# The last tile's 20 nodes: four copies in row quarters of the array in the last attention, and high and low parts stacked in one product of the sums

## The chip, the cores and the metric

The kernel runs on one core of a Trainium2 chip. The metric is the device time of one execution in microseconds (us). Before the change the median of three runs is 2953.96 us (2953.91 to 2956.05).

A core has a matrix engine, TensorE (PE in the profile; PEld is its loading of the fixed operand), a vector engine, VectorE (DVE), a scalar engine, ScalarE (ACT), and a general one, GpSimd (POOL). SyncE (SP) issues DMAs, as ACT and POOL also do. Each engine works through its own queue in order. A product on PE contracts over up to 128 rows, and its result goes to one of the accumulator banks.

## The reference, cut to what matters

Four graph layers on 2708 nodes with 512 features, and one adjacency matrix. Each layer's result is added to its input and normalized.

```python
# layer 0: mean over the first 64 neighbours, two linear maps
keep = Ab & (jnp.cumsum(Ab.astype(jnp.int32), axis=1) <= neibor_num)
nb_sum = keep.astype(X.dtype) @ X
xj = leaky_relu(nb_mean @ W_nb.T + b_nb);  xi = leaky_relu(X @ W_line.T + b_line)
# layer 1: mean over all neighbours, then linear maps
agg = mask @ x / jnp.maximum(deg, 1.0)
# layers 2 and 3: attention with 8 heads; layer 3 has a second attention with one head and an MLP
e = jax.nn.leaky_relu(src[:, :, None] + dst[:, None, :], ALPHA)
e = jnp.where(adj_mask[None, :, :], e, NEG)
attn = jax.nn.softmax(e, axis=-1)
return jnp.einsum('hnm,hmo->hno', attn, Wh)
...
h2 = _gat_heads(x1, mask, Wo[None], ao[None])[0]
out = jax.nn.relu(jax.nn.elu(h2) @ lin1_w + lin1_b) @ lin2_w + lin2_b
```

## The kernel before, in words

The 2708 nodes are cut into 22 tiles: 21 of 128 and a last one of 20 (`few` in the code, `LAST` its number). The transposed mask `maskT` lies in memory as [128 rows, 22 tiles, 2816 columns] of one-byte numbers: row and tile say which neighbour, the column says which node. In the last tile only 20 of 128 rows hold neighbours; the rest are zero.

Stage 0a (0 to 208 us of the profiled span): for each tile t the rows of x are transposed and multiplied by two weights. The first product is what the sums will add up; `keep_y` (L226) splits it into a rounded high part `yH` (ACT, L229) and the remainder `yL` (DVE, L230), both in a reduced format that PE multiplies faster. The second product becomes `u`, stored by POOL (L336). Beside this, 14 mask tiles are loaded by POOL (L257, kept one or two ahead), counted on ACT (L262), cut to 64 neighbours by prefix sums on DVE (L268, L271), transposed on PE (L280) and written by ACT into `maskT` as signs (`turn`, L284). Helper `product` (L232) multiplies; `pe()` fixes the order of PE in this stage.

Stage 0b (208 to 484): the first sums over neighbours (L478). Output tiles go in blocks (tiles 20 and 21 first, then 0 to 3, 4 to 7 and so on). For each neighbour tile j ACT casts a block's mask (`kT`, L351, two buffers) and PE multiplies it by yH and by yL of tile j, for each of the block's tiles into its own bank; there are four such banks. At the block's end ACT copies the banks out (L491). The other 8 masks are prepared between these products.

Stage 1 (484 to 867): the same for layer 1. First the products for yH, yL (L244) with `keep_y`, then per output tile one bank and 22 x 2 products (L529), with masks cast by ACT in three groups (L526). In this stage the last tile's product takes a path of its own (L234 to L242): four products into four column quarters (L237), added up by `groups4`, a matrix that adds four groups of 32 rows (L241).

The attentions with heads follow (to about 2121). Then the projection of the last attention (`project`, L585, without heads): PE multiplies (L643), ACT forms the exponentials `ecol` and `ucol` (L664, L665) and scales the rows into `R2` (L676). POOL then loads the weights of the MLP (L1012, L1013).

The last attention (`last_attention`, L1083) goes over six quads of output tiles (five of 512 columns, one of 148). For each neighbour tile j DVE makes the weights `e` (L722, four buffers) and adds them, scaled, into `acc` (L1101, L1103), and PE multiplies them with the four 128-column parts of R2 into four banks `pn` (L1097). At a quad's end ACT and DVE copy two banks each (L1118, L1116), PE adds up acc over rows (`den`, L1120), DVE takes the reciprocal (L1022), normalizes and applies elu (L1024, L942 to L945), and PE computes the MLP of this quad (L1046, L1071) between the next quad's tiles.

In all these loops the last tile costs PE as much as a full one. Already before the change, the attentions with heads put a second copy of the last tile's 20 rows at rows 32 to 51 (`TWIN` = 32), for which one DMA copies the mask's rows (L567).

The instructions are put into each engine's queue by a scheduler; except where `pe()` or `issue_after` ties them, their order on an engine is not fixed by the text.

Of the kernel before, what the change touches and what calls it, by code (L numbers as in the profile page):

```python
# [9 lines left out]
F32 = mybir.dt.float32  # L10
# [3 lines left out]
AF = mybir.ActivationFunctionType  # L14
OP = mybir.AluOpType
AX = mybir.AxisListType
# [14 lines left out]
def kernel(  # L31
# [18 lines left out]
    def rows(t):  # L50
        return min(P, N - t * P)
# [41 lines left out]


    few = N - (NT - 1) * P
    groups4 = const.tile([P, 32], F32, name="groups4")
    nc.vector.tensor_reduce(groups4, ident.rearrange("p (g n) -> p n g", g=4), AX.X, OP.add)
    assert few <= 32

    behind = []  # L100
# [100 lines left out]
    with ExitStack() as phase:  # L201
# [25 lines left out]

        def keep_y(t, n, pm):
            highs[t] = nc.scalar.copy(yH[:n, t, :], pm[:n])  # L229
            return nc.vector.tensor_sub(yL[:n, t, :], pm[:n], yH[:n, t, :].bitcast(F32))  # L230

        def product(xT, n, w, which, order=as_it_comes, pm=None):  # L232
            pm = ps_mm.tile([P, D], F32, name=f"pm{which}") if pm is None else pm
            if n == few and order is as_it_comes:  # L234
                nc.gpsimd.memset(xT[:, :, n:32], 0.0)
                for k in range(KD):
                    nc.tensor.matmul(pm[32 * k:32 * k + 32], xT[:, k, :32], w[:, k, :], start=True, stop=True)  # L237
                u = sm.tile([P, D], F32, name="u")
                nc.scalar.copy(u, pm)
                pm = sums()  # L240
                nc.tensor.matmul(pm[:few], groups4[:, :few], u, start=True, stop=True)  # L241
                return pm  # L242
            for k in range(KD):
                order(nc.tensor.matmul(pm[:n], xT[:, k, :n], w[:, k, :], start=(k == 0), stop=(k == KD - 1)))  # L244
            return pm


# [25 lines left out]
        def turn(i, m, psum, order=as_it_comes):  # L273
            t, n = turns[i], rows(turns[i])
            for g0 in range(0, NT, G):
                g1 = min(g0 + G, NT)
                ps = psum()
                for j in range(g0, g1):
                    w = rows(j)
                    order(nc.tensor.transpose(ps[:w, j - g0, :n], m[:n, j * P:j * P + w], identb[:n, :n]))  # L280
                parts = [(P, g0, min(g1, FULL))] + ([(rows(FULL), FULL, NT)] if g1 > FULL else [])
                for w, a, b in parts:
                    if a < b:
                        nc.scalar.activation(maskT[:w, a:b, t * P:t * P + n], ps[:w, a - g0:b - g0, :n], AF.Sign,  # L284
                                             saturate=False)
                yield

        def rows_of(src):
# [55 lines left out]
        with ExitStack() as ph:  # L344
# [123 lines left out]
            for i, b in enumerate(cuts):  # L468
                ts_ = range(*b)
                pa = {t: sums() for t in ts_}  # L470
                for j in range(NT):
                    if j + 1 < NT:
                        nxt, nxt_made = kept(b, j + 1)
                    elif i + 1 < len(cuts):
                        nxt, nxt_made = kept(cuts[i + 1], 0)
                    for t in ts_:
                        for y in (yH, yL):
                            nc.tensor.matmul(pa[t], kT[:, (t - b[0]) * P:(t - b[0] + 1) * P], y[:, j, :],  # L478
                                             start=(j == 0 and y is yH), stop=(j == NT - 1 and y is yL))
                    kT = nxt  # L480
                    if j % 3:
                        next(todo, None)
                    with tc.issue_after(nxt_made.ins):
                        next(both, None)
                with tc.issue_after(nxt_made.ins):
                    reciprocals(slice(*b))
                us = {}
                for t in ts_:
                    n = rows(t)
                    us[t] = st.tile([P, D], F32, name=f"u{t - b[0]}")  # L490
                    nc.scalar.activation(us[t][:n], pa[t][:n], AF.Copy, scale=rkeep[:n, t:t + 1])  # L491
                todo = finish(ts_, us)
# [23 lines left out]
        with ExitStack() as ph:  # L516
            st = ph.enter_context(tc.tile_pool(name="l1b", bufs=2))
            for t in range(NT):
# [4 lines left out]
                for g0 in range(0, NT, G):  # L523
                    g1 = min(g0 + G, NT)
                    mf = st.tile([P, G, P], F32R, name="mf")
                    nc.scalar.copy(mf[:, :g1 - g0, :], maskT[:, g0:g1, t * P:(t + 1) * P])  # L526
                    for j in range(g0, g1):
                        for y in (yH, yL):
                            nc.tensor.matmul(pa, mf[:, j - g0, :], y[:, j, :],  # L529
                                             start=(j == 0 and y is yH), stop=(j == NT - 1 and y is yL))  # L530
                u = sm.tile([P, D], F32, name="u")
                nc.vector.scalar_tensor_tensor(u[:n], pa[:n], rdeg[:n, t:t + 1], z1, op0=OP.mult, op1=OP.add)
                nc.vector.scalar_tensor_tensor(u[:n], u[:n], 0.0, x1, op0=OP.max, op1=OP.add)
# [29 lines left out]
        nc.vector.tensor_reduce(pick_c[:, g], rows_c, AX.X, OP.add)  # L563


    LAST, TWIN = NT - 1, 32
    nc.sync.dma_start(maskT[TWIN:TWIN + few, LAST, :N], maskT[:few, LAST, :N])  # L567
    ucol = late.tile([P, NT, H], F32, name="ucol")
    ecol = late.tile([P, NT, H], F32, name="ecol")
    for c in (ucol, ecol, vcol, bcol):  # L570
# [17 lines left out]
    def project(name, source, layer, v_dram, cuts, turned=None, first=None):  # L588
# [12 lines left out]
        with ExitStack() as ph:  # L601
# [24 lines left out]
            for t in range(NT):  # L626
# [8 lines left out]
                if twice:  # L635
                    nc.gpsimd.memset(xT[:, :, n:TWIN], 0.0)
                    nc.gpsimd.tensor_copy(xT[:, :, TWIN:TWIN + n], xT[:, :, :n])
                elif t == LAST:
                    nc.gpsimd.memset(R2[TWIN:2 * TWIN, LAST, :], 0.0)
                m = TWIN + n if twice else n  # L640
                for k in range(KD):
                    for a in range(2):
                        nc.tensor.matmul(pm[a][:m, :D // 2 + heads], xT[:, k, :m], w[:, k, a, :D // 2 + heads],  # L643
# [17 lines left out]
                            nc.vector.tensor_mul(view(R2[at, t, a * D // 2:(a + 1) * D // 2]), view(pm[a][at, :D // 2]),  # L661
                                                 ecol[at, t, a * hh + k:(a + 1) * hh:2, None].to_broadcast([n, hh // 2, HO]))
                else:
                    nc.scalar.activation(ecol[:n, t, :heads], d, AF.Exp, scale=ALPHA)  # L664
                    nc.scalar.activation(ucol[:n, t, :heads], d, AF.Exp, scale=1.0 - ALPHA)  # L665
                with tc.issue_after(scaled[t - 1].ins) if first and t else nullcontext():
                    made = first(t) if first else None
                for a in range(0 if twice else 2):
                    to, src = R2[:n, t, a * D // 2:(a + 1) * D // 2], pm[a][:n, :D // 2]
                    if heads > 1:  # L670
                        with tc.issue_after(made.ins) if made else nullcontext():
                            scaled[t] = nc.vector.tensor_mul(to.rearrange("p (h o) -> p h o", h=hh),
                                                             src.rearrange("p (h o) -> p h o", h=hh),
                                                             ecol[:n, t, a * hh:(a + 1) * hh, None].to_broadcast([n, hh, HO]))
                    else:
                        scaled[t] = nc.scalar.activation(to, src, AF.Copy, scale=ecol[:n, t, 0:1])  # L676
                if heads > 1:
                    nc.scalar.activation(vcol[:n, t, :], b[:n, :], AF.Exp, scale=ALPHA - 1.0)
                    nc.gpsimd.tensor_scalar(bcol[:m, t, :], ucol[:m, t, :], -STEP * (1.0 + 2.0 ** -22), None,
# [404 lines left out]
    def last_attention(ph, att, last):  # L1084
# [4 lines left out]
        for b, (t0, t1) in enumerate(quads):  # L1089
# [4 lines left out]
            for j in range(NT):  # L1094
                e = att.weights(b, 0, j, v)
                for k in range(KD):
                    nc.tensor.matmul(pn[k][:, :w], R2[:, j, k * P:(k + 1) * P], e[:, :w],  # L1097
                                     start=(j == 0), stop=(j == NT - 1))

                if j == 0:  # L1100
                    nc.vector.tensor_scalar(acc[:, :w], e[:, :w], ecol[:, j, 0:1], None, op0=OP.mult)  # L1101
                else:
                    nc.vector.scalar_tensor_tensor(acc[:, :w], e[:, :w], ecol[:, j, 0:1], acc[:, :w],  # L1103
                                                   op0=OP.mult, op1=OP.add)

                if b == 1 and j == 4:
# [361 lines left out]
```

## Time and profile before

| what | us |
| --- | --- |
| median of three runs | 2953.96 |
| lowest and highest run | 2953.91, 2956.05 |
| span of the profiled execution, first to last instruction | 2955.5 |
| stage 0a, to 208.2: PE busy | 193.3 |
| 484.5 to 647.4 (products of layer 1): PE busy | 158.6 of 162.9 |
| 866.9 to 2121.0 (attentions with heads): PE busy | 1220.2 of 1254.1 |
| 2121.0 to 2238.7 (projection of the last attention): PE busy | 113.4 of 117.7 |
| 2910.0 to 2955.5 (the end): PE busy | 31.2 of 45.5 |

The profiled execution has no time of its own beside its span; it lies 1.5 us above the median of the runs. The mean granted clock of PE is 0.995 of full speed. In a row of the profile, the line number is that of the kernel, then come engine, operation, output and inputs by name, shapes and count; in brackets stands how long the engine was idle before and what ended that. Matmuls are pipelined, so the spacing of their starts is shorter than the duration of one.

### The profile page before, as it was taken

What the parts mean: (1) busy time and instruction counts of PE and PEld (TensorE: products, weight loads), DVE (VectorE), ACT (ScalarE), POOL (GpSimd) and SP (SyncE); (2) the same over time, 40 slices, a digit from 0 to 9 for tenths busy, and PEclk for the clock granted to TensorE, in tenths of its full rate; (3) what the DMA queues carried; (4) which work ended last, traced back from release to release, by engine and by line L of the source; (5) the groups of instructions that cost most, each with busy time, mean ns of one, the idle gap of its engine ahead of it and who ended that gap; (6) DMA issues with size and microseconds to landing.
All of it is one profiled execution on the core that took longest, in us unless ns stands there. A gap on an engine that the chain in (4) does not pass through costs nothing. (4 is left out here: it accounts for less than half of the span.)

```text
span 2955.5 us, 36461 instructions
## 1 busy us (share of the span) xinstructions
PE 2874.1 (97%) x14398; PEld 1606.6 (54%) x14398; DVE 1998.5 (68%) x2408; ACT 1515.0 (51%) x1759; POOL 207.4 (7%) x344
## 2 busy tenths in 40 slices
PE   8999999999999999999999999999999999999998
PEld 4557766458888343444466433444475555555555
DVE  5866637543334999999977999999953434444342
ACT  3646532113223999999965999999951000000001
POOL 1101101101110000000022000000000010000001
PEclk9999999999999999999999999999999999999999
DMA  4633426322222111111143111121161000000000
GB/s 128 130 87 72 107 79 185 118 65 86 83 72 82 35 40 39 38 45 44 35 138 134 40 40 39 41 65 37 33 157 61 4 25 15 25 15 16 15 20 22
DMA packets 121152, 185.59 MB, mean 63 GB/s; under 512 B 41741, under 2 KB 66562, under 8 KB 120972
## 3 DMA queue, kind: packets, MB, share of 16 engines
q1 hardware_dynamic: 91808, 121.57, 13.8%
q0 software_dynamic: 18160, 57.39, 6.8%
q10 hardware_dynamic: 11004, 4.22, 0.6%
q8 instruction: 115, 1.88, 0.3%
q14 instruction: 65, 0.53, 0.1%
HBM read 153.10 MB, written 44.65 MB: 67 GB/s over the span
## 5 line engine op out<-in xcount | busy, mean ns | idle before, releaser
L722 DVE SCALAR_TENSOR_TENSOR e<-v_bc,ucol,maskT 128x1408 f32<-128x1408 f32 (+3 forms) x804 | 1135.9, 1469 | 327.6 <-PE pn L1097 314.4
L749 ACT ACTIVATE c<-e,bcol 128x1300 fp8e4<-128x1300 f32 (+1 forms) x688 | 965.8, 1423 | 65.4 <-DVE e L722 21.8
L916 PE MATMUL po<-e,R 128*64 128x512 f32 (+2 forms) x4224 | 907.8, 549 | 30.2 <-DVE e L722 27.3
L916 PEld LDWEIGHTS po<-e,R 128*64 128x64 f32 x4224 | 343.0, 137 | 561.9 <-issue 387.2
L1097 PE MATMUL pn<-e,R 128*128 128x512 f32 (+1 forms) x1056 | 413.4, 542 | 0.0
L1097 PEld LDWEIGHTS pn<-e,R 128*128 128x128 f32 x1056 | 191.0, 190 | 199.3 <-issue 196.1
L1048 ACT ACTIVATE w<-pl,b 128x256 f32<-128x256 f32 (+1 forms) x88 | 41.0, 466 | 372.8 <-PE pl L1046 364.7
L478 PE MATMUL acc<-yH,kT 128*128 128x512 f32 x484 | 197.4, 408 | 4.6 <-ACT kT L351 4.6
L478 PE MATMUL acc<-yL,kT 128*128 128x512 f32 x484 | 189.2, 391 | 0.0
L529 PE MATMUL acc<-yH,mf 128*128 128x512 f32 x484 | 188.4, 389 | 0.0
L529 PE MATMUL acc<-yL,mf 128*128 128x512 f32 x484 | 188.3, 389 | 0.0
L643 PE MATMUL pm<-w,xT 128*128 128x264 f32 (+1 forms) x704 | 167.5, 391 | 2.4 <-POOL ln_rs L120 0.8
L244 PE MATMUL pm<-weight,xT 128*128 128x512 f32 (+1 forms) x344 | 158.3, 603 | 7.6 <-DVE u L334 6.8
L1046 PE MATMUL pl<-lin 128*128 128x256 f32 (+1 forms) x704 | 153.4, 371 | 3.7 <-DVE lin L945 3.7
L120 POOL TENSOR_TENSOR ln_rs<-ln_rs,half 128x1 f32<-128x1 f32 (+1 forms) x88 | 55.1, 627 | 1447.1 <-DVE ln_rs L119 1378.6
L1071 PE MATMUL pl<-lin,w 128*128 128x512 f32 x336 | 150.8, 593 | 0.0
L1046 PEld LDWEIGHTS pl<-lin 128*128 128x128 f32 x704 | 129.1, 190 | 34.5 <-issue 15.8
L526 ACT CAST mf<-maskT 128x1024 fp32r<-128x1024 fp8e4 (+1 forms) x66 | 64.5, 977 | 156.5 <-PE acc L529 152.9
L643 PEld LDWEIGHTS pm<-w,xT 128*128 128x128 f32 (+1 forms) x704 | 129.2, 189 | 27.7 <-ACT xT L133 3.0
L244 PE MATMUL pm<-w,xT 128*128 128x512 f32 x296 | 135.3, 600 | 6.0 <-DVE yL L230 3.1
L351 ACT ACTIVATE kT<-maskT 128x512 fp32r<-128x512 fp8e4 (+1 forms) x132 | 77.5, 593 | 118.1 <-PE acc L478 118.1
L818 PE MATMUL pd<-c,parts_c 128*12 128x384 fp8e4 (+2 forms) x2752 | 128.3, 307 | 0.0
(239 smaller groups left out, 2635.4 us busy)
## 6 DMA issues: line engine op xcount, KB each, us to landing
rows<-x_dram SPq DMA_DIRECT2D x63, 256.0 KB
v_bc<-v_dram SPq DMA_DIRECT2D x16, 704.0 KB
rows<-in_x_dram SPq DMA_DIRECT2D x42, 256.0 KB
x_dram<-u POOLq DMA_DIRECT2D x42, 256.0 KB, 2.4
v_bc<-v_dram SPq DMA_DIRECT2D x16, 650.0 KB
m<-in_adj_dram POOLq DMA_DIRECT2D x13, 677.0 KB, 6.9
r_dram<-u POOLq DMA_DIRECT2D x21, 256.0 KB, 2.3
rows<-r_dram SPq DMA_DIRECT2D x21, 256.0 KB
```

The source lines that it names most:

```text
L244: order(nc.tensor.matmul(pm[:n], xT[:, k, :n], w[:, k, :], start=(k == 0), stop=(k == KD - 1)))
L351: made = nc.scalar.activation(kT[:, :w], maskT[:, j, b[0] * P:b[0] * P + w], AF.Relu, scale=-1.0)
L478: nc.tensor.matmul(pa[t], kT[:, (t - b[0]) * P:(t - b[0] + 1) * P], y[:, j, :], start=(j == 0 and y is yH), stop=(j == NT - 1 and y is yL))
L529: nc.tensor.matmul(pa, mf[:, j - g0, :], y[:, j, :], start=(j == 0 and y is yH), stop=(j == NT - 1 and y is yL))
L643: nc.tensor.matmul(pm[a][:m, :D // 2 + heads], xT[:, k, :m], w[:, k, a, :D // 2 + heads], start=(k == 0), stop=(k == KD - 1))
L722: self.made = nc.vector.scalar_tensor_tensor(e[:, :w], v[:, :w], ucol[:, j, h:h + 1], maskT[:, j, c0:c0 + w], op0=OP.max, op1=OP.mult)
L749: nc.scalar.activation(c[:, :w], e[:, :w], AF.Sigmoid, bias=bcol[:, j, h:h + 1], scale=STEP, saturate=False)
L818: pe(nc.tensor.matmul(p[32 * g:32 * g + 12, :c1 - c0], parts_c[:, j, h, :], c[:, c0:c1], start=(i == 0 and h == hs[0]), stop=(i == NT - 1 ...
L916: pe(nc.tensor.matmul(po[i][HO * k:HO * k + HO, :c1 - c0], R2[:, j, h * HO:(h + 1) * HO], e[:, c0:c1], start=(i_ == 0), stop=(i_ == NT - 1)))
L1046: nc.tensor.matmul(pl[:, :w], self.lin1[:, k, f * P:(f + 1) * P], h[:, k, :w], start=(k == 0), stop=(k == KD - 1))
L1071: nc.tensor.matmul(pl[:n], gT[:, f, (t - t0) * P:(t - t0) * P + n], self.lin2[:, f, :], start=(f == 0), stop=(f == KF - 1))
L1097: nc.tensor.matmul(pn[k][:, :w], R2[:, j, k * P:(k + 1) * P], e[:, :w], start=(j == 0), stop=(j == NT - 1))
```

## The change

In the sums, the last tile's low parts move under its high parts: `keep_y` writes the rounded high part to rows 0 to 19 of yH, and the remainder to rows 32 to 51 of yH (through a second rounded copy in yL at those rows). For this the projection has to give the same 20 rows twice: `product` doubles the columns of the transposed input by a memset and a copy on POOL, or uses a `groups4` of twice the width. The mask's 20 rows are copied to rows 32 to 51 by one POOL DMA for each of the 22 mask tiles, as soon as a tile is turned. Then one product takes the place of two for j = LAST, in both sums.

In the last attention the last tile's rows stand four times, at rows 0, 32, 64 and 96: in the mask (two more DMAs on SP), in the projection's input (three memsets and three copies on POOL), and so in R2, ecol and ucol. For j = LAST the four products for the four parts of R2 each contract over 32 rows of their own, instead of all 128. `acc` takes the 20 rows once.

```diff
@@ -93,8 +93,10 @@
-    groups4 = const.tile([P, 32], F32, name="groups4")
-    nc.vector.tensor_reduce(groups4, ident.rearrange("p (g n) -> p n g", g=4), AX.X, OP.add)
+    LAST, TWIN = NT - 1, 32
+    groups4 = const.tile([P, 64], F32, name="groups4")
+    for i in range(2):
+        nc.vector.tensor_reduce(groups4[:, 32 * i:32 * i + 32], ident.rearrange("p (g n) -> p n g", g=4), AX.X, OP.add)
...
         def keep_y(t, n, pm):
             highs[t] = nc.scalar.copy(yH[:n, t, :], pm[:n])
+            if t == LAST:
+                low = slice(TWIN, TWIN + n)
+                nc.scalar.copy(yL[low, t, :], pm[low])
+                return nc.vector.tensor_sub(yH[low, t, :], pm[low], yL[low, t, :].bitcast(F32))
             return nc.vector.tensor_sub(yL[:n, t, :], pm[:n], yH[:n, t, :].bitcast(F32))
+
+        def halves(j):
+
+            return (yH,) if j == LAST else (yH, yL)
...
-                nc.tensor.matmul(pm[:few], groups4[:, :few], u, start=True, stop=True)
+                nc.tensor.matmul(pm[:TWIN + few], groups4[:, :TWIN + few], u, start=True, stop=True)
                 return pm
+            m = n
+            if n == few:
+                m = TWIN + n
+                nc.gpsimd.memset(xT[:, :, n:TWIN], 0.0)
+                nc.gpsimd.tensor_copy(xT[:, :, TWIN:m], xT[:, :, :n])
             for k in range(KD):
-                order(nc.tensor.matmul(pm[:n], xT[:, k, :n], w[:, k, :], start=(k == 0), stop=(k == KD - 1)))
+                order(nc.tensor.matmul(pm[:m], xT[:, k, :m], w[:, k, :], start=(k == 0), stop=(k == KD - 1)))
             return pm
...
@@ -283,6 +298,9 @@
+                if g1 == NT:
+                    nc.gpsimd.dma_start(maskT[TWIN:TWIN + few, LAST, t * P:t * P + n],
+                                        maskT[:few, LAST, t * P:t * P + n])
                 yield
...
                     for t in ts_:
-                        for y in (yH, yL):
+                        for y in halves(j):
                             nc.tensor.matmul(pa[t], kT[:, (t - b[0]) * P:(t - b[0] + 1) * P], y[:, j, :],
-                                             start=(j == 0 and y is yH), stop=(j == NT - 1 and y is yL))
+                                             start=(j == 0 and y is yH), stop=(j == LAST))
...
                     for j in range(g0, g1):
-                        for y in (yH, yL):
+                        for y in halves(j):
                             nc.tensor.matmul(pa, mf[:, j - g0, :], y[:, j, :],
-                                             start=(j == 0 and y is yH), stop=(j == NT - 1 and y is yL))
+                                             start=(j == 0 and y is yH), stop=(j == LAST))
...
-    LAST, TWIN = NT - 1, 32
-    nc.sync.dma_start(maskT[TWIN:TWIN + few, LAST, :N], maskT[:few, LAST, :N])
+    for g in (2, 3):
+        nc.sync.dma_start(maskT[g * TWIN:g * TWIN + few, LAST, :N], maskT[:few, LAST, :N])
...
                 elif t == LAST:
-                    nc.gpsimd.memset(R2[TWIN:2 * TWIN, LAST, :], 0.0)
-                m = TWIN + n if twice else n
+                    for g in range(1, 4):
+                        nc.gpsimd.memset(xT[:, :, g * TWIN - TWIN + n:g * TWIN], 0.0)
+                        nc.gpsimd.tensor_copy(xT[:, :, g * TWIN:g * TWIN + n], xT[:, :, :n])
+                m = n if t < LAST else TWIN + n if twice else 3 * TWIN + n
...
-                    nc.scalar.activation(ecol[:n, t, :heads], d, AF.Exp, scale=ALPHA)
-                    nc.scalar.activation(ucol[:n, t, :heads], d, AF.Exp, scale=1.0 - ALPHA)
+                    d2 = d if m == n else pm[1][:m, D // 2:D // 2 + heads]
+                    nc.scalar.activation(ecol[:m, t, :heads], d2, AF.Exp, scale=ALPHA)
+                    nc.scalar.activation(ucol[:m, t, :heads], d2, AF.Exp, scale=1.0 - ALPHA)
...
-                    to, src = R2[:n, t, a * D // 2:(a + 1) * D // 2], pm[a][:n, :D // 2]
+                    to, src = R2[:m, t, a * D // 2:(a + 1) * D // 2], pm[a][:m, :D // 2]
...
-                        scaled[t] = nc.scalar.activation(to, src, AF.Copy, scale=ecol[:n, t, 0:1])
+                        scaled[t] = nc.scalar.activation(to, src, AF.Copy, scale=ecol[:m, t, 0:1])
...
                 for k in range(KD):
-                    nc.tensor.matmul(pn[k][:, :w], R2[:, j, k * P:(k + 1) * P], e[:, :w],
+                    at = slice(k * TWIN, k * TWIN + TWIN) if j == LAST else slice(0, P)
+                    nc.tensor.matmul(pn[k][:, :w], R2[at, j, k * P:(k + 1) * P], e[at, :w],
                                      start=(j == 0), stop=(j == NT - 1))
 
+                n = rows(j)
...
-                    nc.vector.scalar_tensor_tensor(acc[:, :w], e[:, :w], ecol[:, j, 0:1], acc[:, :w],
+                    nc.vector.scalar_tensor_tensor(acc[:n, :w], e[:n, :w], ecol[:n, j, 0:1], acc[:n, :w],
                                                    op0=OP.mult, op1=OP.add)
```

## The prediction

> **What bounds the kernel now.** I began with the page's head and its engine row, to see which engine could pay for anything at all.
>
> ```profile
> span 2955.5 us, 36461 instructions
> PE 2874.1 (97%) x14398; PEld 1606.6 (54%) x14398; DVE 1998.5 (68%) x2408; ACT 1515.0 (51%) x1759; POOL 207.4 (7%) x344
> ```
>
> TensorE (PE) is 97% busy, so time on any other engine counts only where PE waits for it. Next, the busy time by windows, for the three stretches in which the change removes PE work: the first sums over neighbours, the second ones, the last attention. Columns: stretch, length, then busy time of PE, PEld, DVE, ACT, POOL.
>
> ```profile
> 208.20:484.50 276.30, 270.28 (x1245) 203.73 (x1245) 161.96 (x254) 136.69 (x215) 29.25 (x43) 1.00 0.40 103
> 647.40:866.90 219.50, 219.50 (x969) 181.74 (x969) 66.33 (x129) 62.42 (x64) 24.50 (x43) 1.00 0.24 78
> 2238.70:2910.00 671.30, 667.62 (x2000) 368.23 (x2000) 291.75 (x450) 55.85 (x112) 48.78 (x57) 1.00 0.06 18
> ```
>
> The second sums have no PE gap; their 968 products come every 219.5 / 968 = 0.227 us, though a row of the groups gives one 0.389 us: products overlap, so spacing and not duration is the price. Then the timeline at the places where the removed work stands. At the end of a block of four tiles in the first sums:
>
> ```profile
> 277.61 0.63 ACT L351 ACTIVATE kT<-maskT 128x512 fp32r<-128x512 fp8e4 x1 [1.18 <-PE acc L478]
> 278.15 2.41 ACT L491 ACTIVATE u<-acc,rkeep 128x512 f32<-128x512 f32 x4
> ...
> 280.37 0.40 PE L478 MATMUL acc<-yL,kT 128*128 128x512 f32 x1
> ...
> 280.61 0.50 PE L478 MATMUL acc<-yH,kT 128*128 128x512 f32 x1
> ```
>
> ScalarE (ACT) casts the next mask, then empties four banks one by one until 280.56; PE, which writes those banks anew, starts the last at 280.61. At the end of a group of four tiles (a quad) in the last attention:
>
> ```profile
> 2443.42 1.64 DVE L1103 SCALAR_TENSOR_TENSOR acc<-e,ecol,acc 128x512 f32<-128x512 f32 x1
> 2443.49 0.59 ACT L1118 COPY lin<-pn 128x512 f32<-128x512 f32 x1 [31.28 <-PE pn L1097]
> 2444.98 0.68 DVE L1116 COPY lin<-pn 128x512 f32<-128x512 f32 x1
> ...
> 2445.86 1.02 PE L1120 MATMUL den<-acc,ones 128*128 128x512 f32 x2
> ...
> 2446.06 0.69 DVE L1116 COPY lin<-pn 128x512 f32<-128x512 f32 x1 [0.41 <-PE pn L1097]
> 2446.67 0.74 DVE L722 SCALAR_TENSOR_TENSOR e<-v_bc,ucol,maskT 128x512 f32<-128x512 f32 x1
> 2446.72 1.02 PE L1097 MATMUL pn<-e,R 128*128 128x512 f32 x2
> 2447.33 3.35 DVE L1022 RECIPROCAL rc<-den 128x512 f32<-128x512 f32 x1
> ```
>
> Here VectorE (DVE) has little slack. After these copies it works without a break until the fifth mask tile of weights is made, at 2458.67 + 0.74 = 2459.4; PE, with four tiles of 3.43 us from 2446.72, wants it at 2460.4. Only 1.0 us is spare.
>
> **What the skill says.** (1) "TensorE: Matmul & The Clock Gate", Part 3: row tiles of 32 rows run side by side, four at 512 columns measured 3.07 times faster than one after the other. No row tiles exist in the trace of before, but column tiles do, in this data type:
>
> ```profile
> 641.97 1.06 PE L237 MATMUL pm<-w,xT 128*32 128x512 f32 x8
> ...
> 643.38 1.43 PE L237 MATMUL pm<-weight,xT 128*32 128x512 f32 x8 [0.35 <-POOL xT L235]
> ...
> 644.27 1.02 PE L241 MATMUL acc<-u,groups 128*20 128x512 f32 x2
> ```
>
> Eight records (four products, two records each) start within 0.43 us; in the second set the next product follows 0.89 us after the first start. (2) "TensorEngine Tiling (Array Packing)", Key Properties: a change of tiling mode drains TensorE. The trace agrees: 641.97 is 0.09 us later than the beat of 0.43 us, and the way back costs about 0.2 us. (3) "GPSIMD Engine Reference", Specifications: it shares its SBUF interfaces with VectorE. The L1103 row above takes 1.64 us while POOL adds rows, 0.75 us elsewhere.
>
> **Second sums (L529): -5.0 us.** Each of 22 output tiles has one product fewer, 22 x 0.227. ACT's mask casts (1.05 us) and DVE's reading of another bank lie beside it; nothing is late next.
>
> **First sums (L478): -1.1 us of 5.0.** 22 x 0.228 = 5.0 is removed. But in three of the six block ends (278, 323, 368) ACT's row of cast and four copies starts when the product of the tile *before* the last ends, which doesn't move; PE's start at 280.61 stays. Those three give nothing. The first (234.42) waits for the kT cast, also unmoved. The end at 439 has a different product behind it (3.4 us, which covers the copies): 4 x 0.228 = 0.9 is kept. At 484 the next product waits for ACT behind four copies, and their start can come one product earlier: 0.2. Between 0.5 and 3.
>
> **Last attention (L1097): -7.9 us.** Records of 512 columns come every 0.429 us, so the four products of the last tile take 8 x 0.429 = 3.43 us. In quarters: two waves 0.89, drains 0.3, in all 1.15 to 1.2 (the page's factor gives 3.43 / 3.07 = 1.12, an estimate). Bounds: 0.86 (no drains) to 3.75 (no overlap, drains added). PE gains 2.28 per full quad. What follows:
> - End of quad 0 (2312): DVE is free at 2312.7, its two bank copies end 1.27 us earlier, the fifth tile comes at 2326.6 and PE wants it at 2326.7: all 2.28 kept.
> - Quads 1 to 3 (as above): the banks are full at 2443.6, but DVE is in its 1.64 us row until 2445.06. Its copies end at 2446.28 instead of 2446.75; its whole chain moves up 0.47 us. PE, 2.28 early, waits for the second bank (0.4) and then for the fifth tile, which is there at 2459.0 instead of 2460.44 for PE's old start: 1.44 each, 4.3 for three.
> - Quad 4: the next quad is 148 wide, PE runs dry and already waits 2.8 us for DVE (L945); only DVE's shift counts, 0.8.
> - Quad 5: 8 x 0.13 = 1.03 becomes about 0.55: 0.5; 13.9 us of other products cover what follows.
> Sum 2.28 + 4.3 + 0.8 + 0.5 = 7.9. If DVE's order puts the copies ahead, all five keep 2.28: 11.9. With no overlap: +1.8.
>
> **What is added: +1.5 us.** First projection: the last tile's rows are doubled on POOL before each of its two products. The first pair lies beside PE (input there at 196.7, PE comes at 201.25). The second pair must wait for the first product: 204.86 + 0.16 + memset 0.14 + copy 0.25 (rows L636, L637) + 0.1 = 205.5, not 204.69: 0.9 with the wait. If POOL's queue puts the first pair behind the store at 203.07, 2.9 more. Second layer: a further ACT copy of 0.57 before the copy for which PE waits at 646.43: 0.5. Projection of the last attention: six short POOL steps can run from 2216.3, PE wants them at 2233.2: 0.1; behind the weight load that waits until 2233.45 they would cost 3. The doubled reduction at the start (0.38) lies before 3.5 us of DVE idleness, the second mask DMA on SP at 861.7 before an idle SP. Row counts of 116 in place of 20 change no duration: the 20-row casts take 0.57, the 128-row ones 0.59.
>
> 22 mask copies go into POOL's queue, each waiting for ACT's L284. A POOL issue is 0.55 us, a landing of the stores there 2.3; the reader, ACT's cast of the last mask tile (L351), now waits for them, and behind it on ACT stand the four bank copies and so PE. But it reads a block only long after: the masks of the last block are made by 381 and read near 480. At nothing, unless they stand ahead of a mask load, see below. The two attentions with heads keep their instructions; the extra mask rows there meet rows of zeros.
>
> **Sum:** -5.0 - 1.1 - 7.9 + 1.5 = -12.5 against the profiled span, 2955.5 to 2943.0. The median of the runs shown, 2953.96, is 1.5 below that span; the same difference gives 2941.5.
>
> **Rivals.**
> Fuller recovery (DVE copies ahead, block ends keep 3): -5 - 3 - 11.9 + 1 = -18.9, 2935. For it: engines' orders are not the text's (the second stage's mask load at 198.25 runs before the first stage's store at 203.07), so they may shift. Against: DVE's rows were ready earlier in this order too.
> Little gained: quarters don't overlap, or two covers are lost (2.9 and 3): -5 - 1.1 + 1.8 + 1.5 = -2.8, 2951. Against: L237. For: row tiles aren't in the trace.
> Slower: mask copies hold up mask loads on POOL.
>
> ```profile
> 120.05 0.72 POOL L257 DMA_DIRECT2D m<-in_adj_dram  x1
> 120.32 2.64 ACT L284 ACTIVATE maskT<-acc 128x1024 fp8e4<-128x1024 bf16 x4
> 126.84 2.55 ACT L262 ACTIVATE m<-m,gate 128x2708 bf16<-128x2708 bf16 x1
> ```
>
> A load lands after 6.9 us and is used after 6.8: no slack. A copy ahead of it waits for L284 until 122.96, 3.5 us with its issue. Six loads are that tight (56, 101, 110, 120, 154, 164), delays 2.4 + 4.4 + 3.7 + 3.5 + 4.4 + 3.4 = 21.8, and DVE's prefix sums behind them leave PE no reserve: -12.5 + 20.5 = +8, 2962. It decides from 12.5 / 6 = 2.1 us each. Against: the load needs only the transposes and is ready before L284 begins, so it should be queued first.
>
> **Chances.** Forecast 0.54 (2938 to 2947), fuller 0.16, little 0.16, slower 0.14. The range 2934 to 2952 leaves out the last. A measurement of this kernel tells about 0.2% (5.9 us) from no change: faster 0.70, same 0.16, slower 0.14.
>
> **What would show it.** L529's stretch shorter by 5.0 us; L478's by 1; quads 1 to 3 by 1.4 each with PE waiting for DVE's e; the eight quarter records in two waves. POOL copies before L257 in its order, or records of the last tile spaced 0.43 us one by one, would prove me wrong.

## The result, and the profile after

The changed kernel takes 2942.66 us (median of four runs, 2939.28 to 2943.7), the kernel before, run beside it, 2955.01 (2953.91 to 2957.62): a ratio of 0.9953, 95% interval 0.9941 to 0.9965, 12.35 us less. The forecast was 2941.5, or 12.5 less. The interval is about 7 us wide, so this agreement says little about the terms of the sum.

The page of the changed kernel begins like this; PE is as full as before, with 19.6 us less of it.

```profile
span 2937.5 us, 36437 instructions
...
PE 2854.5 (97%) x14354; PEld 1590.3 (54%) x14354; DVE 1996.9 (68%) x2409; ACT 1515.0 (52%) x1761; POOL 220.2 (7%) x375
```

The two profiled spans differ by 18.0 us, more than the medians. So I cut both by the starts of PE's rows and asked of every piece whether other profiles repeat it.

| stretch on PE | before | after | difference | forecast |
| --- | --- | --- | --- | --- |
| start to the last tile's first product of stage 0a | 201.25 | 199.09 | -2.2 | none |
| from there to the last product of the first sums | 282.85 | 279.9 | -2.95 | +0.9 - 1.1 = -0.2 |
| products of layer 1 | 163.3 | 164.0 | +0.7 | +0.5 |
| second sums, first start to last | 219.3 | 214.3 | -5.0 | -5.0 |
| attentions with heads, projections | 1372.1 | 1368.7 | -3.4 | -0.1 to +0.1 |
| last attention, first product to last `den` | 670.2 | 664.3 | -5.9 | -7.9 |
| from there to the end | 46.6 | 47.2 | +0.6 | none |

Two rows are chance. The -2.2 arises in the first 25 us, where one set of eight products took 5.40 us in the one execution and 3.70 in the other; later profiles of changed kernels show both. The -3.4 stands in a row that took 1374.0 us in a second profile of the same changed kernel (`after_again` below), and between 1369.5 and 1376.0 us over the eleven profiles of the experiments, in none of which the attentions with heads are touched. Part of it is PE's clock: near 1500 us it is halved for 6.8 us in the profile of before and in `after_again`, and not in that of the changed kernel. Without these two rows, 12.4 us remain, about what the medians say.

The +0.6 in the last row is not chance. The stretch takes 47.0 to 47.4 us in the nine profiles of kernels whose first sums are changed, and 46.4 to 46.5 in the four others. It arises after the last store has been issued; its cause was not looked for. So the stretches to explain are the first sums, which gave more than forecast, and the last attention, which gave less.

The same three stretches by windows, in the changed kernel (columns: stretch, length, busy time of PE, PEld, DVE, ACT, POOL, then PE's clock, the DMA share and GB/s). Note the clock of 0.99 in the last line; before it was 1.00 there.

```profile
199.09:479.50 280.41, 273.76 (x1240) 200.98 (x1240) 163.78 (x257) 137.27 (x216) 33.95 (x55) 1.00 0.40 105
643.00:857.50 214.50, 214.50 (x947) 177.61 (x947) 66.38 (x129) 62.44 (x64) 24.47 (x43) 1.00 0.25 80
2226.00:2891.00 665.00, 660.54 (x1999) 362.75 (x1999) 289.65 (x450) 55.24 (x112) 48.77 (x57) 0.99 0.05 18
```

The end of a quad in the last attention, from the timeline of the changed kernel (start, duration, engine and line, in brackets the wait before and what ended it):

```profile
2427.62 0.31 PEld L1119 LDWEIGHTS pn<-e,R 32*128 32x128 f32 x8 [0.76 <-DVE xT L124]
2427.73 0.75 DVE L743 SCALAR_TENSOR_TENSOR e<-v_bc,ucol,maskT 128x512 f32<-128x512 f32 x1 [0.32 <-PE pn L1119]
2428.51 1.64 DVE L1126 SCALAR_TENSOR_TENSOR acc<-e,ecol,acc 128x512 f32<-128x512 f32 x1
...
2428.69 1.12 PE L1143 MATMUL den<-acc,ones 128*128 128x512 f32 x2
2428.78 1.07 ACT L1141 COPY lin<-pn 128x512 f32<-128x512 f32 x2 [31.48 <-PE pn L1119]
...
2430.08 1.27 DVE L1139 COPY lin<-pn 128x512 f32<-128x512 f32 x2
2430.81 0.30 PEld L1119 LDWEIGHTS pn<-e,R 128*128 128x128 f32 x2 [0.96 <-DVE lin L1139]
2431.28 0.73 DVE L743 SCALAR_TENSOR_TENSOR e<-v_bc,ucol,maskT 128x512 f32<-128x512 f32 x1
2431.94 3.34 DVE L1043 RECIPROCAL rc<-den 128x512 f32<-128x512 f32 x1
```

The eight quarter records take 1.07 us from first load to `den`, where they took 3.43. But PE then stands before a bank that DVE hasn't emptied: DVE is in its 1.64 us row until 2430.15, as before.

A good ruler for this stage is the time from one `den` to the next. Before: 131.48 to 131.49 four times, then 68.60 for the short last quad. After: 129.32, 130.10, 130.11, 130.11, then 71.31. Up to the fifth `den` that is 8.6 us less, and the last step gives 2.7 of them back. The timeline of PE there:

```profile
2819.01 1.13 PE L1143 MATMUL den<-acc,ones 128*128 128x512 f32 x2
...
2820.73 4.14 PE L1119 MATMUL pn<-e,R 128*128 128x148 f32 x30 [0.35 <-DVE lin L1139]
...
2828.22 6.68 PE L1067 MATMUL pl<-lin 128*128 128x256 f32 x16 [3.35 <-DVE lin L966]
```

Sixteen records of 256 columns take 6.68 us. In the kernel before, the same sixteen came as 12 in 2.86 us and, after a wait, 4 in 1.13. Asked for the clock microsecond by microsecond (the column after POOL), the profile of the changed kernel answers:

```profile
2826.00:2827.00 1.00, 0.00 (x0) 0.00 (x0) 1.00 (x4) 0.41 (x1) 0.00 (x0) 1.00 0.03 8
2827.00:2828.00 1.00, 0.00 (x0) 0.00 (x0) 1.00 (x3) 0.74 (x2) 0.00 (x0) 0.71 0.00 0
2828.00:2829.00 1.00, 0.78 (x2) 0.69 (x3) 1.00 (x3) 0.00 (x0) 0.00 (x0) 0.50 0.00 0
...
2833.00:2834.00 1.00, 1.00 (x4) 0.74 (x3) 1.00 (x5) 0.00 (x0) 0.00 (x0) 0.50 0.00 0
```

PE's clock was halved for 6.8 us, from 0.8 us before the end of PE's wait of 3.35 us. The kernel before waits 2.79 us at this place, and its clock stays at 1.00:

```profile
2848.16 2.86 PE L1046 MATMUL pl<-lin 128*128 128x256 f32 x12 [2.79 <-DVE lin L945]
```

### The profile page after: what moved, and what is told of

It reads as the page before. It is cut to its first block, busy times and chain, and to the rows that moved or that the text cites. A ratio compares the mean times of both kernels' runs of the same rounds, so it can differ in the third digit from the quotient of the medians.

```text
span 2937.5 us, 36437 instructions
## 1 busy us (share of the span) xinstructions
PE 2854.5 (97%) x14354; PEld 1590.3 (54%) x14354; DVE 1996.9 (68%) x2409; ACT 1515.0 (52%) x1761; POOL 220.2 (7%) x375
## 5 line engine op out<-in xcount | busy, mean ns | idle before, releaser
L1119 PE MATMUL pn<-e,R 128*128 128x512 f32 (+3 forms) x1056 | 403.0, 545 | 1.1 <-DVE lin L1139 0.3
L1119 PEld LDWEIGHTS pn<-e,R 128*128 128x128 f32 (+1 forms) x1056 | 183.9, 190 | 197.1 <-issue 181.5
L496 PE MATMUL acc<-yL,kT 128*128 128x512 f32 x462 | 180.7, 391 | 0.0
L547 PE MATMUL acc<-yL,mf 128*128 128x512 f32 x462 | 179.7, 389 | 0.0
L259 PE MATMUL pm<-w,xT 128*128 128x512 f32 x296 | 133.6, 594 | 5.3 <-ACT xT L135 2.1
```

What stands on the lines that cost most here:

```text
L259: order(nc.tensor.matmul(pm[:m], xT[:, k, :m], w[:, k, :], start=(k == 0), stop=(k == KD - 1)))
L547: nc.tensor.matmul(pa, mf[:, j - g0, :], y[:, j, :], start=(j == 0 and y is yH), stop=(j == LAST))
L1119: nc.tensor.matmul(pn[k][:, :w], R2[at, j, k * P:(k + 1) * P], e[at, :w], start=(j == 0), stop=(j == NT - 1))
```

## Experiments

Theory A at the outset: the parts are independent; in the last attention DVE's chain at the quads' ends (slow row, bank copies, next weights, reciprocal) takes over from PE, and at quad 4 the longer wait costs the clock; in the first sums something that the forecast didn't see makes the block ends cheaper. Rivals: the forecast's own prices hold and the rest is chance; or the ends are ruled by something else than DVE's copies.

**The parts alone.** `sums_only` has the last attention as before (full 128-row products for j = LAST, one mask DMA), `quarters_only` has the sums as before.

> The two sums as in the changed kernel, the last attention as before. Theory A (the parts are independent, each is worth what its stage shows in the two traces): second sums -5.0 us (22 products of a low part fewer, 0.227 us each), first sums -2.8 (blocks of 43.6/44.3/44.3/70.8/43.1 us against 43.9/44.9/44.8/71.2/44.1), layer 1's products +0.6, the last attention's ends 131.5 us apart as before: 7.2 us below the kernel before, about 2947.8. Rival B (the prediction's own price for the first sums, -1.1 net of nothing, and +0.9 for POOL's copy ahead of them; the rest of what the trace shows there is chance): 4.5 to 5 us below, about 2950.

> The last attention's four quarters alone, the sums as before. Theory A: the ends come 129.3, 130.1, 130.1, 130.1 us apart instead of 131.5, the last 68.5 instead of 71.3 less 2.7 (71.3): about 5.4 us below the kernel before, 2949.6, and together with the sums alone the whole 12.4. Rival B (part of the gain of the quarters hangs on the sums, or the parts hide each other): the two gains together differ from 12.4 by more than 2 us.

Measured: 2950.46 us for the sums (ratio 0.9978, 0.9972 to 0.9984) and 2949.87 for the quarters (0.9976, 0.9968 to 0.9985), beside 2956.61 for the kernel before: -6.2 and -6.7, together 12.9 against the 12.4 of the whole. The parts add up; neither needs the other. Each missed its own number: the sums lie between their theory (-7.2) and its rival (-4.5 to -5), and half a microsecond of what is missing is the longer end of the kernel, which the 7.2 left out; the quarters gave 1.3 more than the 5.4 expected. In `sums_only` the steps between `den`s are 131.48 to 131.49 and 68.60 again and the second sums 214.4; in `quarters_only` they are 129.32, 130.11, 130.10, 130.10. The one surprise is its last step: 70.03, not the 71.3 expected, which accounts for the 1.3. The wait is the same 3.35 us; the clock was halved for 3.4 us instead of 6.8:

```profile
2842.65 5.41 PE L1050 MATMUL pl<-lin 128*128 128x256 f32 x16 [3.35 <-DVE lin L949]
```

**First sums as before, second ones stacked.** In `second_only` stage 0a makes y of the last tile as before (no doubling on POOL), the first sums loop over both parts for every tile, and one DMA on SP copies the mask's rows during the products of layer 1:

```diff
-                if g1 == NT:
-                    nc.gpsimd.dma_start(maskT[TWIN:TWIN + few, LAST, t * P:t * P + n],
-                                        maskT[:few, LAST, t * P:t * P + n])
...
-                        for y in halves(j):
+                        for y in (yH, yL):
...
+                if t == 3:
+                    nc.sync.dma_start(maskT[TWIN:TWIN + few, LAST, :N], maskT[:few, LAST, :N])
```

> The changed kernel with the first sums as before: high and low parts under each other only from layer 1 on, no 22 mask copies on POOL, one on SP instead. Theory A (the first sums' change is worth what the traces show, -2.8): 2.8 us slower than the changed kernel, about 2945.5. Rival B (the prediction: -1.1 in the first sums, +0.9 in the stage ahead of them): 0.2 us slower, the same within the measurement, and the edit could be left out.

Measured: 2946.42 us, ratio 0.9966 (0.9955 to 0.9978). Next to 0.9953 and 0.9961 of the changed kernel in its two comparisons that is 1.5 to 4 us slower, though the intervals overlap. The stretch is clearer: from the first bank copies of the first sums to their last product it takes 249.8 us before, 249.5 here, 246.4 in the changed kernel and in `sums_only`. But 0.7 us of this is only PE's last product coming sooner; the next stage's first product waits for ACT, which stands behind the last bank copies (2.95 us after their start before, 2.96 after). From the first bank copies to the last ones it is 248.9 us before, 248.5 here, 246.1 in the other two. So the change is worth 2.4 to 2.8 us in the first sums, more than twice the 1.1 forecast, and the 0.7 comes back as the +0.7 in the row of layer 1.

**Why.** At 276, 321 and 365 us the block ends in PE's timeline of the changed kernel look like this:

```profile
275.48 1.07 PE L496 MATMUL acc<-yH,kT 128*128 128x512 f32 x4
276.39 0.56 PE L295 MATMUL pm<-identb,w 128*128 128x128 bf16 x7
277.00 0.50 PE L496 MATMUL acc<-yH,kT 128*128 128x512 f32 x1
277.34 0.39 PE L496 MATMUL acc<-yL,kT 128*128 128x512 f32 x1
277.57 0.23 PE L295 MATMUL pm<-identb,w 128*128 128x128 bf16 x1
277.61 0.47 PE L496 MATMUL acc<-yH,kT 128*128 128x512 f32 x1
```

Transposes of the next mask (L295) stand just where PE waits for ACT to empty the banks. In the kernel before they come 24 products later. Their line in the text didn't move; the scheduler put them elsewhere once the products had changed. `turns_apart` fixes PE's order in the first sums to that of the text:

```diff
-                            nc.tensor.matmul(pa[t], kT[...], y[:, j, :], start=(j == 0 and y is yH), stop=(j == LAST))
+                            pe(nc.tensor.matmul(pa[t], kT[...], y[:, j, :], start=(j == 0 and y is yH), stop=(j == LAST)))
...
-                    for _ in turn(i, m, lambda: next(psum)):
+                    for _ in turn(i, m, lambda: next(psum), pe):
```

> The changed kernel with PE's order in the first sums fixed to that of the text: the transposes of the next mask come 24 products after a block's end, as in the kernel before, and none at the end itself. Theory A (what the first sums gained beyond the prediction's 1.1 us is transposes that moved into the wait for the bank copies at three block ends): the stretch from the last product of the stage before to the last of the first sums is 275 to 275.5 us instead of 272.6, the whole 2 to 3 us longer than the changed kernel. Rival B (with a product fewer in the last tile the block ends are shorter by themselves): 272.6 to 273, no difference.

Measured: 274.2 us for that stretch, 1.6 more than in the changed kernel; the 2.4 or more of the expectation was too much. The median, 2944.26, is that of the changed kernel beside it (2944.24): times can't tell 1.5 us. The trace can. A block end without the transposes:

```profile
279.06 1.07 PE L496 MATMUL acc<-yH,kT 128*128 128x512 f32 x4
280.58 0.50 PE L496 MATMUL acc<-yH,kT 128*128 128x512 f32 x1 [0.45 <-ACT u L509]
```

PE waits for ACT's copies. From one block's bank copies to the next:

| | block 2 | 3 | 4 | 5 | 6 |
| --- | --- | --- | --- | --- | --- |
| before | 43.88 | 44.86 | 44.84 | 71.20 | 44.12 |
| text's order | 43.86 | 44.89 | 44.88 | 70.87 | 43.13 |
| changed | 43.59 | 44.29 | 44.29 | 70.81 | 43.12 |

In the text's order blocks 2 to 4 keep their old length to 0.04 us although each lost four products: at these ends ACT is the bound, as forecast. In the changed kernel the transposes fill the wait, and each gives 0.3 to 0.6. Block 5 tells nothing: with the first sums as before it takes 70.7 to 71.2 us in four profiles. The text's order shows another term too, which the scheduler had hidden:

```profile
202.47 3.64 PE L259 MATMUL acc<-w,xT 128*52 128x512 f32 x8
206.61 3.64 PE L259 MATMUL pm<-weight,xT 128*52 128x512 f32 x8 [0.50 <-POOL xT L257]
```

PE waits for POOL's doubling of the second input: 4.14 us between the two products here, 3.44 before. In the changed kernel two products of the first sums (0.66 us) stand in that gap.

**DVE's part at the quads' ends.** `act_copies` puts the copies of all four banks on ACT; `act_again` is the same kernel beside `after_again`, the changed one.

```diff
             for k in range(KD):
-                if k % 2:
-                    nc.vector.tensor_copy(sums[k], pn[k][:, :w])
-                else:
-                    nc.scalar.copy(sums[k], pn[k][:, :w])
+                nc.scalar.copy(sums[k], pn[k][:, :w])
```

> The changed kernel with all four bank copies of the last attention on ACT, none on DVE. Theory A (at the ends of quads 1 to 4 the quarters hand the wait to DVE: PE waits first for DVE's bank copies and then for e behind the copies and the reciprocal; ACT has been idle 31 us there): 0.8 us less for each of quads 1 to 3, and at quad 4 1.3 us from the shorter chain, after which PE waits 2.1 us instead of 3.35 for the hidden layer and keeps its clock, 1.8 us more: 5.5 us below the changed kernel, about 2937. Rival B (four copies one after the other on ACT, 0.53 to 0.59 us each, hold the banks as long as two on each engine): 0 to 1 us slower than the changed kernel.

> The changed kernel once more, as the measure for the three beside it on the same chip: 0.4 to 0.5% below the kernel before. If the halved TensorE clock at the end of quad 4 hangs on when a free-running window ends and not on the kernel, the stretch from the fifth to the last sum of divisors is here something between 69.5 us (no halving) and 71.3 (6.8 us of it), not the same again.

> All four bank copies on ACT once more, now beside the changed kernel. Theory A (DVE's chain was the wait): the five full steps between the sums of divisors are 129.3 us each and the last 67.7, as in its first run, and the median is about 6 us below that of the changed kernel's second run (4 x 0.78 at the quads' ends and 3.6 or 2.3 at the last). Rival B (that run's gain against the kernel before was the chip's): within 2 us of it.

Measured: 2939.69 us (0.9941, 0.9928 to 0.9954) for `act_copies` and 2937.34 (0.9935, 0.992 to 0.9949) for `act_again`, beside which the changed kernel took 2944.24 (0.9961, 0.9947 to 0.9976). All four steps between full quads are 129.31 or 129.32, the last 67.72, with a wait of 1.69 us (2.1 expected) and no halved clock. The last attention is 658.3 us long against 663.0 in `after_again`: 4.7 us are this edit's, and the other 2.2 of the 6.9 are not shown to be. The end of a quad in `act_again`, PE without a wait:

```profile
2431.40 1.64 DVE L1126 SCALAR_TENSOR_TENSOR acc<-e,ecol,acc 128x512 f32<-128x512 f32 x1
2431.58 1.12 PE L1140 MATMUL den<-acc,ones 128*128 128x512 f32 x2
2431.66 2.05 ACT L1138 COPY lin<-pn 128x512 f32<-128x512 f32 x4 [31.48 <-PE pn L1119]
2432.54 5.74 PE L1119 MATMUL pn<-e,R 128*128 128x512 f32 x13
```

Four copies on ACT take 2.05 us together, and PE doesn't wait for them. This version beats both kernels: its five times beside the changed kernel's (2934.41 to 2939.56) all lie below them (2943.74 to 2948.22). In `after_again` the last step was 70.03: so how long the clock stays halved differs between profiles of one kernel.

Is that edit worth something without the quarters? `before_act` makes it in the kernel before.

> The kernel before, with nothing of the change, and all four bank copies of the last attention on ACT. Theory A (DVE's copies became the wait only with the quarters; before, PE was the wait at quads 0 to 3): the full steps stay at 131.5 us, and only the last, in which PE waited 2.8 us for DVE, shrinks from 68.6 to about 67.3. Rival B (the copies on ACT are worth 0.8 us at each end in any kernel): 130.7 us for the full steps.

Measured, in one profile: 131.48 to 131.49 for the full steps, 67.55 for the last. So DVE became the wait only with the quarters; before, PE was.

Which part of DVE's chain is it? `no_row_add` drops one line of the MLP, so that POOL doesn't add while DVE makes its row:

```diff
-                nc.gpsimd.tensor_add(x3s[t], x3s[t], self.b2[:n])
```

> The changed kernel without POOL's addition of the second layer's bias to the rows (the output lacks that bias). Theory A (the ends of quads 1 to 3 keep only part of the gain because DVE's row of weighted sums takes 1.64 us while POOL adds, and the bank copies stand behind it): the row takes 0.75 us, and the steps between the sums of divisors go from 130.1 to 129.3 us. Rival B (it is DVE's chain of copies, e and reciprocal as such): 130.1 us stay, or go by less than 0.2.

Measured, in one profile: 129.32 for all full steps, and 69.19 for the last (3.21 us of wait, and again a halved clock). The row is short:

```profile
2436.76 0.75 DVE L1125 SCALAR_TENSOR_TENSOR acc<-e,ecol,acc 128x512 f32<-128x512 f32 x1
2436.94 1.12 PE L1142 MATMUL den<-acc,ones 128*128 128x512 f32 x2
2437.02 1.07 ACT L1140 COPY lin<-pn 128x512 f32<-128x512 f32 x2 [31.48 <-PE pn L1118]
2437.43 1.28 DVE L1138 COPY lin<-pn 128x512 f32<-128x512 f32 x2
```

So the 0.78 us that quads 1 to 3 left lying came from the slow row in front of the copies; taking either out of the chain is enough.

**The clock.** `warm` has eight products that nobody reads in front of the hidden layer after quad 4:

```diff
+                if t0 == NT - 6 and f == 0:
+                    for _ in range(8):
+                        nc.tensor.matmul(pl[:, :P], ones, ones, start=True, stop=True)
                 for k in range(KD):
                     nc.tensor.matmul(pl[:, :w], self.lin1[:, k, f * P:(f + 1) * P], ...
```

> The changed kernel with eight products of 128 columns of ones, into a bank that the next product overwrites, in front of the hidden layer after quad 4, where PE waits 3.35 us. Theory A (it is that wait which halves TensorE's clock): clock 1.00 through the 16 records behind it, and the last step between the sums of divisors 69.5 us instead of 71.3 or 70.0. Rival B (the records are slow for another reason, the second half of DVE's chain): 70.0 to 71.3, or more by the products' 2 us.

Measured: 69.54 for the last step. The median is 2943.01, which can't be told from the changed kernel's 2944.24. PE's timeline:

```profile
2828.92 1.95 PE L1068 MATMUL pl<-ones 128*128 128x128 f32 x16
2832.43 2.86 PE L1070 MATMUL pl<-lin 128*128 128x256 f32 x12 [1.57 <-DVE lin L966]
2836.18 1.13 PE L1070 MATMUL pl<-lin 128*128 128x256 f32 x4 [0.89 <-DVE lin L966]
```

The sixteen records are back at 2.86 and 1.13 us. PE still starts the hidden layer when DVE lets it; only 1.95 us of its idleness are filled, and the clock holds in this profile, where it was halved in all six with a wait of 3.21 or 3.35 us here. The halving cost 0.5 us (70.03) or 1.8 (71.31).

The length of the wait alone doesn't decide, though. In the kernel before, a wait of 2.82 us elsewhere, in the attentions with heads, ends with a halved clock (the row of PE's timeline, then one microsecond behind it with the clock after POOL's column):

```profile
969.38 2.84 PE L916 MATMUL po<-e,R 128*64 128x512 f32 x4 [2.82 <-DVE e L722]
...
970.00:971.00 1.00, 1.00 (x2) 0.00 (x0) 1.00 (x2) 1.00 (x2) 0.00 (x0) 0.50 0.00 0
```

The wait there is 2.71 to 2.82 us in all thirteen profiles, and in all of them the clock is halved at it or within 2 us. Further on, between 1605 and 1620 us, a wait of 2.58 or 2.59 us is met by a halved clock in ten profiles and by none in three. So 2.79 us at the hidden layer, left alone in two profiles, is not shown to be safe.

**Side by side or merely small?** `one_quarter` takes all four products of the last tile from the first copy:

```diff
-                    at = slice(k * TWIN, k * TWIN + TWIN) if j == LAST else slice(0, P)
+                    at = slice(0, TWIN) if j == LAST else slice(0, P)
```

> The changed kernel with the four products of the last tile all taken from the first copy, rows 0 to 31 of the array, instead of one from each quarter; the copies are made as before and the result is the same. Theory A (the gain is that products in different row quarters run side by side): the eight records come one by one, 3.43 us plus 0.1 to 0.3 for the changes of tiling, and the sums of divisors stand 131.5 to 131.8 us apart, not 129.3 and 130.1. Rival B (32 rows instead of 128 make a product cheaper by themselves): 1.07 us for the eight and 129.3 and 130.1 us, as in the changed kernel.

Measured, in one profile: 134.5, 133.6, 133.9, 133.9 between the `den`s, slower than before by 2.1 to 3.0 us a step where 0.1 to 0.3 were expected. The single time is 2964.61 us, beside 2959.67 for the kernel before. The loads of PE at the end of quad 0, then two microseconds with PE's clock after POOL's column:

```profile
2304.53 0.19 PEld L1119 LDWEIGHTS pn<-e,R 128*128 128x128 f32 x1 [0.24 <-issue]
2305.48 0.29 PEld L1119 LDWEIGHTS pn<-e,R 32*128 32x128 f32 x2 [0.76 <-issue]
2306.02 0.18 PEld L1119 LDWEIGHTS pn<-e,R 32*128 32x128 f32 x1 [0.24 <-issue]
2306.45 0.18 PEld L1119 LDWEIGHTS pn<-e,R 32*128 32x128 f32 x1 [0.24 <-issue]
...
2308.16 0.18 PEld L1119 LDWEIGHTS pn<-e,R 32*128 32x128 f32 x1 [0.24 <-issue]
2309.82 0.50 PEld L1143 LDWEIGHTS den<-acc,ones 128*128 128x128 f32 x2 [1.48 <-issue]
...
2307.00:2308.00 1.00, 1.00 (x4) 0.43 (x3) 0.56 (x2) 0.28 (x1) 0.00 (x0) 1.00 0.00 0
2309.00:2310.00 1.00, 1.00 (x3) 0.17 (x2) 0.07 (x1) 0.00 (x0) 0.00 (x0) 0.50 0.00 0
```

The records of 32 rows in one quarter come one by one, 0.43 us apart, like those of 128 rows: without the other quarters the gain is gone. The excess is the clock. It is halved for 6.8 us from 2308.3, although PE hasn't stopped for a moment, and again at the ends of quads 1 to 4, for 3.4, 3.4, 3.4 and 6.8 us. Half of such a stretch is lost. With that taken out, an estimate from these figures, the steps are 131.8 to 131.9 us, 0.3 to 0.4 above the kernel before: the two changes of tiling cost about what was expected.

## Why the prediction was right

The direction and the main mechanisms were right: a product fewer for each tile is worth its spacing, the quarters run side by side, and DVE's slow row takes over as the wait. That the sum came within 0.2 us is luck: the first sums gave more than put, the last attention less, and the two errors cancelled.

- **Second sums, -5.0**: 219.3 to 214.3. Spacing times count was the right price.
- **First sums, -1.1**: that ACT bounds three block ends was right, as blocks 2 to 4 in the text's order show. What failed is the premise that PE's order at the ends stays: "Those three give nothing". With transposes in the wait they gave 1.4. The other two ends came as put: from the last tile's first product to the next block's first, 4.97 us became 4.20 at 439 (0.8 of the 0.9), and the copies at 484 start one product sooner (0.2). In all 2.4 to 2.8 in place of 1.1.
- **Doubling on POOL, +0.9**: 0.7 in the text's order, and next to nothing in the changed kernel, where two other products cover it.
- **Layer 1, +0.5**: from the last tile's first product to the second sums 5.43 us became 6.31, so +0.9. The whole stretch, counted from the bank copies ahead of it, didn't change (164.2 both times), so something else in it gave 0.9; that was not looked for.
- **The quarters' set, 1.15 to 1.2 us**: 1.07 from first load to `den`. Net of both changes of tiling it saves 2.16 us (131.48 to 129.32) where 2.28 was put: two waves of 0.43 and 0.4 for the changes, put at 0.3. "TensorE: Matmul & The Clock Gate" of the Trainium skill, Part 3, has a factor of 3.07; here it is 3.43 / 1.07 = 3.2 from load to load, and 2.7 with both changes counted.
- **Quad 0 all of it, quads 1 to 3 1.44 each**: 2.16, and 1.38 three times. The stated cause, DVE's slow row ahead of its copies, is what `no_row_add` and `act_again` confirm.
- **Quads 4 and 5, 0.8 and 0.5**: right as long as the clock holds; then the stage gives 7.6 (`warm`: 662.5 us), close to the 7.9. PE's full gain at quad 4 is there at the fifth `den`, and the wait for DVE behind it goes from 2.79 to 3.35 us. With the clock halved there, the stage gave 7.1 or 5.9. The forecast had the wait but not what it does to the clock.
- **The end of the kernel, nothing**: it grew by 0.6, see above.
- **Mask copies at nothing, and the rival in which they delay mask loads**: in POOL's timeline of the changed kernel the copies (L302) stand behind the loads (L272), not ahead of them, so what was to decide for that rival isn't there:

```profile
63.61 0.58 POOL L354 DMA_DIRECT2D r_dram<-u  x1 [6.52 <-DVE u L195]
64.18 0.73 POOL L272 DMA_DIRECT2D m<-in_adj_dram  x1
64.89 0.54 POOL L302 DMA_DIRECT2D maskT<-maskT  x1
```

Two slips had no effect on the sum: the delays of that rival add up to 21.8 us, and it was reckoned with 20.5; and the eight records at 641.97 start within 0.48 us, not 0.43.

The Trainium skill's page just named, Part 1, says that TensorE's clock is halved after an idle window of about 3.4 us and that the window runs free, not tied to the kernel. The lengths fit: between the first 20 us and the end of the kernel every halved stretch of these profiles lasts 3.4 or 6.8 us. That a wait has to be as long as the window doesn't: 2.82 us in the kernel before was enough. That the same wait is followed by 3.4 us, by 6.8 or by none would fit a window that runs free, but no run sets its phase. The halved clock at 969 us stood in the profile of before, so the risk of a longer wait at quad 4 could have been put in the forecast.

## What to carry to other kernels

When PE gets faster at a place where it shares a hand-over with another engine, list what that engine does before it reaches the shared buffer; the copies may belong on an engine that is idle there. Where PE already waits more than 2 us, a gain ahead of that wait lengthens it, and may cost the clock behind it as well; look in the profile for the clock after waits of that length. A forecast for a scheduled kernel should ask which ready work could slide into each wait; a removal that was put at nothing may gain from that.

## What the runs showed of the hardware

- Products that use only one 32-row quarter of PE, 0.43 us apart without a gap, were followed by a halved clock at all five ends of full quads in `one_quarter` (2.8 to 4.2 us after the first of their loads), though PE counted as fully busy. With the four quarters side by side that didn't appear, but there the set takes only 1.07 us, so this is no control. That the share of the array counts for the clock is a reading of this one profile, not tested further.
- Going from 128-row to 32-row products, the next load comes 0.95 us after the last one instead of 0.43, in `one_quarter` as in the changed kernel. What the changes there and back cost together is less, 0.3 to 0.4 us, an estimate from the steps between the `den`s.
- Waits of PE of 2.6 to 2.8 us were met by a halved clock at some places and not at others; the halved stretch was 3.4 or 6.8 us long and cost 0.5 or 1.8 us at the hidden layer.
- DVE's weighted-sum row takes 1.64 us while POOL adds and 0.75 without: in `no_row_add` no row over 1 us is left.
- Profiles of one kernel differ by some 2 us at the start alone (`act_copies` and `act_again`), and by 5.3 us in the attentions with heads (the changed kernel and `after_again`). A comparison of two single profiles must be made stage by stage.
